# Query chains of a cross-attention, cut in two: three products in one turn of a pair, four in the other

## The chip, the cores and the metric

One core of a Trainium2 chip runs the whole kernel in one launch. The metric is the device time of that launch in microseconds (us). The engines named below work side by side, each in the order of its own instruction queue: PE (matrix products, results in PSUM banks), ACT (ScalarE: copies out of PSUM, exponentials), DVE (VectorE: maxima, reductions, transposes), POOL (GpSimd: elementwise work on SBUF tiles) and SP, which issues the transfers. Differences of under 0.2% are about what a measurement of this kernel cannot tell from no change.

## The reference

The input x is 8 sequences of 224 tokens, 512 wide; the context is 8 sequences of 750 tokens, 384 wide. Three blocks follow each other, each added to x and followed by a layer norm: self-attention with 16 heads, cross-attention with 16 heads of 64, and a gated feed-forward whose weights are rounded to three values. The change lies in the cross-attention:

```python
q = split_heads(x @ Wq)          # 512 -> 1024
k = split_heads(context @ Wk)    # 384 -> 1024
v = split_heads(context @ Wv)
sim = jnp.einsum('bhid,bhjd->bhij', q, k) * SCALE
attn = jax.nn.softmax(sim, axis=-1)
out = jnp.einsum('bhij,bhjd->bhid', attn, v)
return merge_heads(out) @ Wo + bo
```

## The kernel before

The cross-attention runs from about 492 to 1484 us of the span, as 32 turns (`TURNS`, the loop from `for t in range(-1, TURNS)` on; turn -1 only prepares). Eight turns work on a pair of sequences: turn t has pair p = t // 8, a group g of four heads and u = t % 2, the sequence of the pair. An even and an odd turn with the same g share their queries, so they are called a pair of turns here.

In a turn, PE first does the weighted values of the turn before (`weighted`, L1341, tile ov_c), then the scores of this turn (`scores`, L1229, tile sc_c, 24 matrix products, each recorded as two matmuls), then the products for this turn's values (v_x, v_z, v_w, L1090) and the next turn's keys (k_x, k_z, k_w, L1084), interleaved by hand. In this text a turn is counted from its first sc_c matmul to the next turn's first; the weighted values of a turn then lie at its own end. ACT copies scores out of PSUM (L1242), evacuates the products and does the exponentials (L1325), two heads for each of two halves w. DVE takes the maxima of the scores (L1239, L1249 to L1304), subtracts them (L1313), and normalises the turn before (L1249 to L1282 in `inverse_sums`, and L1358). POOL adds up the exponentials (L1328 to L1330) and does the sums within the products (L1122, L1141).

Queries, keys and values are each computed with Strassen-like products of halves: seven products instead of eight, with intermediate sums. `half_steps` writes them as a generator of eight steps, so that the loop can place each step. A product x is copied to m1, then accumulated on and copied to u2, then to u4; z plus m1 is the first block c11; w is copied as c22 (which u4 is added to), goes on to c21 (with u2 added); x ends as c12. The keys' u4 and the queries' u4 are the same buffer, `cku4` (pool `c_sb`, one buffer for each name, `part("k", "u4")`), and the keys' reader of it is the POOL addition at L1141 that makes their c22.

The seven products of the queries (L1097, tiles mq_x, mq_z, mq_w, each product four matmuls in the trace) all stand at the end of each odd turn, for the next two turns. After them comes `ov_c`. Even turns have no query work; their last key step (k_x, then the copy at L1154) stands behind the exponentials in the loop.

Other work is spread over the turns. In turns 0 to 15 ACT sums chunks of the feed-forward weights (L961); from turn 16 on it rounds them (L984), DVE clips them (L990), ACT converts them (L996): one chunk at the opening of each turn and one more at the end of each odd turn, whose conversion follows at the opening of the even turn. From turn 19 and turn 27 on, DVE also normalises finished rows of x (L897, L900). `transpose_x` turns x for the next pair of sequences on PE (L1051) with ACT copies (L1055), in turns 6, 14 and 22; `sum_x` (L1075, four POOL additions) follows it behind `sum_context` (L708). `cross_project` (L262) does the output projection of finished rows in turns 7, 8, 15, 16, 23, 24 and 31.

The PE, ACT, DVE and POOL orders are those in which the code issues (`manual_schedule`); PSUM tiles named "mm" rotate through seven banks. SP's order is chosen by the scheduler.

## Time and profile before

| | us |
|---|---|
| median of 3 runs | 1641.7 (1641.07 to 1641.97) |
| the profiled execution | 1639.92 |
| its span, first to last instruction | 1638.1 |
| turn -1 to the first scores of turn 0 | 492.0 to 507.2 |
| first scores of turn 17, 24, 31 | 1017.0, 1227.7, 1435.3 |
| granted TensorE clock, mean | 0.996 |

The busy shares of the page overlap, since the engines run side by side. [...] In the timeline, a line gives the start, the time, engine, line, operation, output<-inputs, shapes and count; square brackets give the idle time of the engine before it and what ended it.

### The profile page before, as it was taken

How to read it: one execution, taken by the hardware profiler on the slowest of the kernel's cores; microseconds unless marked ns; L12 is line 12 of the kernel's file. 1: busy time of each engine (PE TensorE's matmuls, PEld its weight loads, DVE VectorE, ACT ScalarE, POOL GpSimd, SP SyncE). 2: the span in 40 equal slices, each digit the busy share in tenths (PEclk: the TensorE clock that was granted, in tenths of full speed). 3: DMA queues.
4: the chain of work that ended last, by engine and by line, in shares of the span. 5: the costliest groups of instructions: out<-in, count | busy, mean ns of one | idle time of the engine just before them, and what ended most of it. 6: DMA issues, size and time to landing. Idle time of an engine off the chain costs nothing.

```text
span 1638.1 us, 27155 instructions
## 1 busy us (share of the span) xinstructions
PE 1608.9 (98%) x9682; PEld 1145.7 (70%) x9682; DVE 1341.1 (82%) x2831; ACT 1021.4 (62%) x1874; POOL 934.0 (57%) x861
## 2 busy tenths in 40 slices
PE   8999999999999999999999999999999999999998
PEld 5777676667747877876887876877876877764443
DVE  3999897889956798876889867899987899977877
ACT  5667455556416776755676745776765777746663
POOL 4886575665516564674565664574684474651144
PEclk9999999999999999999999999999999999999999
DMA  8115332424204222330221321231341222413343
GB/s 295 46 52 200 94 121 83 145 77 133 77 1 158 82 62 62 104 107 30 72 88 46 106 80 36 83 101 48 112 131 36 83 89 64 144 45 90 65 91 103
DMA packets 143111, 149.14 MB, mean 91 GB/s; under 512 B 41088, under 2 KB 109184, under 8 KB 142592
## 3 DMA queue, kind: packets, MB, share of 16 engines
q1 hardware_dynamic: 142976, 147.40, 29.4%
q8 instruction: 77, 1.26, 0.3%
q14 instruction: 58, 0.48, 0.1%
HBM read 119.85 MB, written 18.87 MB: 85 GB/s over the span
## 4 chain that ended last, share of the span: by engine, by line
PE 74%; DVE 18%; issue 3%; ACT 3%; POOL 1%; DMA 0%; POOLq 0%; SPq 0%; DVEq 0%; ACTq 0%
PE sc_c L1229 9%; PE ov_c L1341 7%; PE mm_co L262 6%; PE mm_f L1505 6%; PE mm_v L544 5%; DVE cpT L1313 5%; PE q_x L470 5%; PE v_x L1090 5%; PE mm_o L669 4%; PE k_x L1084 4%; PE k_w L1084 3%; PE v_w L1090 3%; PE mq_x L1097 3%; PE q_w L470 2%; PE sc_a L571 2%
## 5 line engine op out<-in xcount | busy, mean ns | idle before, releaser
L1328 POOL TENSOR_TENSOR csh<-cpT 125x672 f32<-125x672 f32 x128 | 210.3, 1643 | 104.6 <-DVE cpT L1313 85.4
L1242 ACT COPY cpT<-sc_c 125x448 f32<-125x448 f32 x384 | 194.9, 535 | 43.0 <-DVE xw L1239 24.0
L200 POOL TENSOR_TENSOR nm_i<-nm_q,mhalf 128x28 f32<-128x28 f32 x32 | 157.9, 4935 | 81.7 <-DVE nm_q L519 81.4
L1313 DVE TENSOR_TENSOR cpT<-cpT,mx_b 125x1344 f32<-125x1344 f32 x128 | 192.6, 1545 | 2.8
L1325 ACT ACTIVATE cpT<-cpT 125x1344 f32<-125x1344 f32 x128 | 170.1, 1329 | 38.7 <-DVE cpT L1313 36.3
L1229 PE MATMUL sc_c<-cq,ckT 64*125 64x224 f32 x1536 | 175.5, 364 | 6.9 <-ACT cpT L1242 6.2
L1122 POOL TENSOR_TENSOR cv<-cv,cvmu 125x384 f32<-125x384 f32 x32 | 31.9, 997 | 263.4 <-ACT cv L1121 252.6
L1229 PEld LDWEIGHTS sc_c<-cq,ckT 64*125 64x125 f32 x1536 | 153.6, 185 | 27.7 <-ACT cpT L1242 14.2
L1341 PE MATMUL ov_c<-cpT,cv 125*64 125x224 f32 x1536 | 158.2, 355 | 2.5 <-ACT cpT L1325 2.5
L1341 PEld LDWEIGHTS ov_c<-cpT,cv 125*64 125x64 f32 x1536 | 109.2, 137 | 52.5 <-issue 8.1
L544 PE MATMUL mm_v<-wv,xnT 128*128 128x512 f32 x224 | 100.4, 592 | 0.0
L1505 PE MATMUL mm_f<-ternary,xqT 128*128 128x512 bf16 x448 | 98.8, 379 | 0.8 <-DVE h L1515 0.8
L262 PE MATMUL mm_co<-xattn_Wo,coT 128*128 128x512 f32 x224 | 97.5, 592 | 0.0
L282 ACT ACTIVATE pr<-sc_a 128x448 f32<-128x448 f32 x120 | 57.9, 535 | 60.4 <-PE sc_a L571 60.1
L1329 POOL TENSOR_TENSOR csm<-csh 125x224 f32<-125x224 f32 x128 | 88.9, 695 | 10.0
L1330 POOL TENSOR_TENSOR csm<-csm,csh 125x224 f32<-125x224 f32 x128 | 84.7, 662 | 10.0
L595 DVE TRANSPOSE_TENSOR_REDUCE sm_q<-pr 128x28 f32<-128x896 f32 x64 | 70.6, 1104 | 19.3 <-ACT pr L282 18.9
L669 PE MATMUL mm_o<-attn_Wo,oT 128*128 128x512 f32 x192 | 84.3, 593 | 0.0
L1239 DVE TENSOR_TENSOR xw<-sc_c,cpT 125x448 f32<-125x448 f32 x64 | 36.9, 617 | 55.0 <-PE sc_c L1229 54.5
L1505 PEld LDWEIGHTS <-xqT 128*128 128x128 bf16 x448 | 43.8, 98 | 54.4 <-issue 2.0
L262 PEld LDWEIGHTS mm_co<-xattn_Wo,coT 128*128 128x128 f32 x224 | 42.4, 190 | 50.8 <-issue 50.1
L554 ACT ACTIVATE v<-mm_v,rms_rs 32x512 f32<-32x512 f32 (+2 forms) x80 | 54.4, 681 | 36.7 <-PE mm_v L544 35.9
(237 smaller groups left out, 3931.3 us busy)
## 6 DMA issues: line engine op xcount, KB each, us to landing
w_slot<-qk_sums SPq DMA_DIRECT2D x22, 512.0 KB, 3.6
xw<-w_sums SPq DMA_DIRECT2D x32, 320.0 KB, 3.0
xwq<-xq_sums SPq DMA_DIRECT2D x16, 512.0 KB, 4.2
w_stage<-w_gateT SPq DMA_DIRECT2D x16, 512.0 KB, 4.7
w_stage<-w_upT SPq DMA_DIRECT2D x16, 512.0 KB, 4.8
w_stage<-w_downT SPq DMA_DIRECT2D x16, 512.0 KB, 4.4
tern<-w_t SPq DMA_DIRECT2D x24, 256.0 KB, 2.5
ternary<-tern SPq DMA_DIRECT2D x3, 2048.0 KB, 7.7
```

The lines of the kernel that those rows point to most:

```text
L200: nc.gpsimd.tensor_tensor(y, v, mhalf.to_broadcast([P, v.shape[-1]]), ALU.pow)
L262: nc.tensor.matmul(mm, lhsT=oT[:, k, c : c + P], rhs=w[:, k, :], start=(k == 0), stop=(k == NPAIR - 1),)
L544: nc.tensor.matmul(mm, lhsT=xnT[:, k, at : at + P], rhs=wv[:, k, c * 512 : (c + 1) * 512], start=(k == 0), stop=(k == KD - 1),)
L669: nc.tensor.matmul(mm, lhsT=joint[g][:, hp, :] if at < 0 else o[:, at : at + P], rhs=wo[:, hp, :], start=(hp == 0), stop=(hp == NPAIR - 1),)
L1090: nc.tensor.matmul(mm[:, t, :], lhsT=c[:, t * CT : (t + 1) * CT], rhs=w, start=start and t == 0, stop=True, skip_group_check=True,)
L1229: nc.tensor.matmul(sc[j][:, i, :], lhsT=kT[h0 : h0 + DH, w, ct * CT : (ct + 1) * CT], rhs=q[h0 : h0 + DH, t % 2, w], start=True, stop=True,)
L1242: nc.scalar.copy(pT[:, j, 2 * c2 : 2 * c2 + 2, :], sc[j])
L1313: nc.vector.tensor_tensor(pT[:, j], pT[:, j], nm[:CT, j] .rearrange("p (o q) -> p o q", o=1) .to_broadcast([CT, NCT, S]), ALU.add,)
L1325: nc.scalar.activation(pT[:, j], pT[:, j], AF.Exp)
L1328: nc.gpsimd.tensor_tensor(half, pT[:, j, 0:3], pT[:, j, 3:6], ALU.add)
L1341: nc.tensor.matmul(ov[h0 : h0 + DH, w, :], lhsT=v[:, ct, hq * DH : (hq + 1) * DH], rhs=pTs[w][:, j, ct, :], start=(ct == 0), stop=(ct == N ...
L1505: nc.tensor.matmul(mm, lhsT=xqTs[i][:, k, :], rhs=w[:, k, cols], start=(k == 0), stop=(k == KD - 1),)
```

## The change

The query chain is divided. `queries_opened` runs in even turns (for the next pair of turns): m1, z and the product that becomes u2, then c11. `queries_closed` runs in odd turns: w (c22), the product u4, c21 and c12. What has to survive from one turn to the next are copies in SBUF: c11 in `cq`, now one tile for the whole stage, and u2, which gets S new columns at the end of the `ctx_even` buffer. Since x is no longer accumulated across the two halves, u2 is added to u4 (one more POOL addition), and to c12 on DVE in place of ACT's copy. The last key step of an even turn moves ahead of the exponentials, as it already was in odd turns. `normalise` becomes a generator of two steps, with the query steps between them. `transpose_x` and `sum_x` move from turns 6, 14, 22 (and `sum_x` from behind the context's sums) to the ends of turns 5, 13, 21. Turn -1 runs both halves, one after the other.

```diff
-                ctx_even = wpool.tile([P, CTX], F32, tag="w", name="ctx_even")
+                ctx_even = wpool.tile([P, CTX + S], F32, tag="w", name="ctx_even")
...
+        cq = sb.tile([P, 2, 2, S], F32, name="cq")
+        u2 = ctx_even[:, CTX:]
...
+        def queries_opened():
+            (a11, a12), _ = xblk
+            m1 = part("k", "m1")[:, :S]
+            x_ = query_bank("mq_x")
+            query_product(x_, a11, b11, True)
+            nc.scalar.copy(m1, x_)
+            yield
+            z_ = query_bank("mq_z")
+            query_product(z_, a12, b21, True)
+            query_product(x_, xsum[:, 1], t2, False)
+            nc.scalar.copy(u2, x_)
+            nc.scalar.copy(cq[:, 0, 0], z_)
+            nc.gpsimd.tensor_tensor(cq[:, 0, 0], cq[:, 0, 0], m1, ALU.add)
+            yield
+        def queries_closed():
+            _, (_, a22) = xblk
+            u4 = part("k", "u4")[:, :S]
+            w_ = query_bank("mq_w")
+            query_product(w_, xsum[:, 2], t3, True)
+            nc.scalar.copy(cq[:, 1, 1], w_)
+            x_ = query_bank("mq_x")
+            query_product(x_, xsum[:, 0], t1, True)
+            nc.scalar.copy(u4, x_)
+            nc.gpsimd.tensor_tensor(u4, u4, u2, ALU.add)
+            nc.gpsimd.tensor_tensor(cq[:, 1, 1], cq[:, 1, 1], u4, ALU.add)
+            yield
+            query_product(w_, a22, t4n, False)
+            nc.vector.tensor_tensor(cq[:, 1, 0], w_, u2, ALU.add)
+            query_product(x_, xsum[:, 3], b22, False)
+            nc.vector.tensor_tensor(cq[:, 0, 1], x_, u2, ALU.add)
+            yield
...
-            query = query_steps(t + 1) if t % 2 and t + 1 < TURNS else iter(())
+            query = iter(())
+            if t % 2 == 0 and t + 2 < TURNS:
+                query = queries_opened()
+            elif t % 2 and t + 1 < TURNS:
+                query = queries_closed()
...
-            if t % 2:
-                next(ks, None)
+            next(ks, None)
+            if t < 0:
+                for _ in queries_opened():
+                    pass
             next(query, None)
             if t >= 0:
                 exponentials(t, 1, pTs[1], (0,))
-            if 1 <= t < TURNS - 1:
-                normalise(t - 1, ov)
+            rest = normalise(t - 1, ov) if 1 <= t < TURNS - 1 else iter(())
+            next(rest, None)
             prior = pTs
-            for _ in range(4):
-                next(query, None)
+            for _ in query:
+                pass
+            for _ in rest:
+                pass
             if t >= 0:
                 exponentials(t, 1, pTs[1], (1,))
-            next(ks, None)
-            for _ in query:
-                pass
             weight_work(t, "late")
             if t % 2 and t + 3 < TURNS:
                 load_queries(place(t + 3)[1])
-            if t >= 0 and t % (2 * QG) == 2 * QG - 2 and t + 2 < TURNS:
+            if t % (2 * QG) == 2 * QG - 3 and t + 3 < TURNS:
                 transpose_x(t // (2 * QG) + 1)
+                sum_x()
...
-                if t % 2 == 0:
-                    sum_x()
```

More of the change, by code (lines that the diff above doesn't have):

```diff
@@ L690, in open_context @@
                 t[:, : KC * SC].rearrange("p (k r s) -> p k r s", k=KC, r=2),
-                t[:, KC * SC :].rearrange("p (i s) -> p i s", i=3),
+                t[:, KC * SC : CTX].rearrange("p (i s) -> p i s", i=3),
             )
@@ L1100, in query_product, with half_steps @@
                 )
-        def half_steps(product, a, b, sums_a, sums_b, dest, part, acc, third=None):
+        def half_steps(product, a, b, sums_a, sums_b, dest, part, acc, third):
             (a11, a12), (_, a22) = a
@@ L1111, in half_steps @@
             c11, c12, c21, c22 = (dest(r, c) for r in range(2) for c in range(2))
-            a13, a23, b31, b32, dif = third or (None,) * 5
+            a13, a23, b31, b32, dif = third
             m1, x_ = part("m1"), acc("x")
@@ L1118, in half_steps @@
             product(z_, a12, b21, True)
-            def corner():
-                nc.scalar.copy(c11, z_)
-                nc.gpsimd.tensor_tensor(c11, c11, m1, ALU.add)
-            if third:
-                product(z_, a13, b31, False)
-                corner()
+            product(z_, a13, b31, False)
+            nc.scalar.copy(c11, z_)
+            nc.gpsimd.tensor_tensor(c11, c11, m1, ALU.add)
             yield
@@ L1133, in half_steps @@
             product(w_, s3, t3, True)
-            if third:
-                product(w_, a23, b32, False)
+            product(w_, a23, b32, False)
             nc.scalar.copy(c22, w_)
@@ L1141, in half_steps @@
             nc.gpsimd.tensor_tensor(c22, c22, u4, ALU.add)
-            if not third:
-                corner()
             yield
             product(w_, a22, t4n, False)
-            if third:
-                product(w_, a23, dif, False)
+            product(w_, a23, dif, False)
             yield
@@ L1151, in half_steps @@
             product(x_, s4, b22, False)
-            if third:
-                product(x_, a13, b32, False)
+            product(x_, a13, b32, False)
             nc.scalar.copy(c12, x_)
@@ L1198, in kv_steps, with query_bank @@
             )
-        def query_steps(t):
-            q = qs_[t // 2] = sb.tile([P, 2, 2, S], F32, name="cq")
-            return half_steps(
-                query_product,
-                xblk,
-                ((wq7[:, 0], None), (wq7[:, 1], wq7[:, 2])),
-                [xsum[:, i] for i in range(4)],
-                [wq7[:, 3 + i] for i in range(4)],
-                lambda u, w: q[:, u, w],
-                lambda n: part("k", n)[:, :S],
-                lambda n: ps_mm.tile([P, S], F32, tag="mm", name=f"mq_{n}"),
-            )
+        cq = sb.tile([P, 2, 2, S], F32, name="cq")
+        u2 = ctx_even[:, CTX:]
+        b11, b21, b22 = (wq7[:, i] for i in range(3))
+        t1, t2, t3, t4n = (wq7[:, 3 + i] for i in range(4))
+        def query_bank(name):
+            return ps_mm.tile([P, S], F32, tag="mm", name=name)
+        def queries_opened():
[29 more added lines that the diff above has]
+            yield
         def scores(t):
-            kT, q = kts.pop(t), qs_[t // 2]
+            kT = kts.pop(t)
             pTs = []
@@ L1231, in scores @@
                                 lhsT=kT[h0 : h0 + DH, w, ct * CT : (ct + 1) * CT],
-                                rhs=q[h0 : h0 + DH, t % 2, w],
+                                rhs=cq[h0 : h0 + DH, t % 2, w],
                                 start=True,
@@ L1261, in spread, with normalise @@
             )
-        def inverse_sums(t):
+        def normalise(t, ov):
+            p, g, u = place(t)
             rc, quarter, res = spread("rc_c")
@@ L1275, in inverse_sums @@
                 nc.vector.reciprocal(res[:Q32, j], tot[:, j::2])
-            for g in range(1, P // Q32):
+            for y in range(1, P // Q32):
                 nc.vector.tensor_copy(
-                    res[g * Q32 : (g + 1) * Q32, g // 2], res[:Q32, g // 2]
+                    res[y * Q32 : (y + 1) * Q32, y // 2], res[:Q32, y // 2]
                 )
+            yield
             for j in range(2):
@@ L1287, in inverse_sums @@
                 )
-            return rc
+            c = (2 * p + u) * S % RING
+            n = min(S, RING - c)
+            for at, q, m in ((c, 0, n), (0, n, S - n)):
+                if m:
+                    nc.vector.tensor_tensor(
+                        oT[:, 2 * g : 2 * g + 2, at : at + m], ov[:, :, q : q + m],
+                        rc[:, :, q : q + m], ALU.mult,
+                    )
+            yield
         def maxima(w):
@@ L1349, in weighted @@
             return out
-        def normalise(t, ov):
-            p, g, u = place(t)
-            rc = inverse_sums(t)
-            c = (2 * p + u) * S % RING
-            n = min(S, RING - c)
-            for at, q, m in ((c, 0, n), (0, n, S - n)):
-                if m:
-                    nc.vector.tensor_tensor(
-                        oT[:, 2 * g : 2 * g + 2, at : at + m], ov[:, :, q : q + m],
-                        rc[:, :, q : q + m], ALU.mult,
-                    )
         def cross_project(i, k0, k1):
@@ L1394, in decoder_block @@
             done.setdefault(t + 1, []).append(i)
-        kts, vs, qs_, outs = {}, {}, {}, {}
+        kts, vs, outs = {}, {}, {}
         pTs = prior = None
@@ L1409, in decoder_block @@
                 if t == TURNS - 1:
-                    normalise(t - 1, ov)
+                    for _ in normalise(t - 1, ov):
+                        pass
                 nm = maxima(1)
@@ L1433, in decoder_block @@
                 exponentials(t, 1, pTs[1], (0,))
-            if 1 <= t < TURNS - 1:
-                normalise(t - 1, ov)
+            rest = normalise(t - 1, ov) if 1 <= t < TURNS - 1 else iter(())
+            next(rest, None)
             prior = pTs
-            for _ in range(4):
-                next(query, None)
+            for _ in query:
+                pass
+            for _ in rest:
+                pass
             if t >= 0:
                 exponentials(t, 1, pTs[1], (1,))
-            next(ks, None)
-            for _ in query:
-                pass
             weight_work(t, "late")
@@ L1479, in decoder_block @@
             cross_project(i, 0, NPAIR - 2)
-        normalise(TURNS - 1, ov)
+        for _ in normalise(TURNS - 1, ov):
+            pass
         for i in last:
```

## The prediction

> **What bounds the kernel now.** I read the page first, for the shares; then a table by turns, for idle PE; then the timeline of the ends of an even turn (10) and an odd one (11), where the edit lies; last the late turns and the granted clock.

> ```profile
> PE 1608.9 (98%) x9682; PEld 1145.7 (70%) x9682; DVE 1341.1 (82%) x2831; ACT 1021.4 (62%) x1874; POOL 934.0 (57%) x861
> ```

> PE is the bound, and the edit removes none of its products: it can only move or end idle time. By turns (10, 11, 20, 21):

> ```profile
> core 0: us, PE busy (x) PEld busy (x) DVE busy (x) ACT busy (x) POOL busy (x), PEclk, DMA share, GB/s
> 800.56:825.59 25.03, 24.77 (x186) 19.55 (x184) 21.17 (x45) 17.84 (x31) 12.48 (x14) 1.00 0.17 53
> 825.59:855.18 29.59, 29.59 (x214) 24.43 (x213) 25.38 (x54) 20.60 (x39) 19.90 (x22) 1.00 0.28 87
> 1102.28:1127.99 25.71, 25.30 (x186) 19.59 (x184) 23.66 (x50) 20.45 (x33) 12.92 (x14) 1.00 0.31 87
> 1127.99:1163.42 35.43, 32.54 (x214) 26.49 (x213) 31.56 (x61) 21.70 (x38) 20.40 (x22) 0.90 0.23 68
> ```

> The even turn is 4.56 us shorter and has an idle PE, the odd one has none. In turns 20 and 21 DVE is nearly full and PE loses far more, with a lower clock. The end of turn 10:

> ```profile
> 818.70 1.43 PE L1084 MATMUL k_x<-ctx_odd,xw 128*128 128x375 f32 x4
> 820.05 2.86 PE L1341 MATMUL ov_c<-cpT,cv 125*64 125x224 f32 x26
> 823.18 2.48 PE L1341 MATMUL ov_c<-cpT,cv 125*64 125x224 f32 x22 [0.26 <-ACT cpT L1325]
> ```

> After 26 matmuls of ov_c PE waits for the last exponential: the starts are 3.13 us apart where 26 times 0.095 is 2.47. That is what three products here would cover. The end of turn 11:

> ```profile
> 845.09 0.92 PE L1097 MATMUL mq_x<-xT,xwq 128*128 128x224 f32 x4
> ...
> 847.05 0.98 POOL L1141 TENSOR_TENSOR ckT<-ckT,cku 128x375 f32<-128x375 f32 x1
> ...
> 849.13 0.35 ACT L1140 COPY cku<-mq_x 128x224 f32<-128x224 f32 x1 [0.47 <-PE mq_x L1097]
> ...
> 850.49 4.76 PE L1341 MATMUL ov_c<-cpT,cv 125*64 125x224 f32 x48
> ```

> Here the POOL line matters: it reads the keys' `cku4` and is done at 848.03, 1.1 us before the queries' u4 copy (L1140) overwrites that buffer. So far nobody waits.

> **Even turns.** From the first score to the end of k_x is 19.40 us (turn 10: 800.56 to 818.70, plus 4 times 0.315). A query product takes 0.756 us (4 starts 0.189 apart), ov_c to the next score 4.69 (850.49 to 855.18), the handover 0.10. So an even turn becomes 19.40 + 3 x 0.756 + 0.10 + 4.69 = 26.46, if nothing waits. Does it? ACT must do, after the first product starts: m1's copy at +1.01 (845.09 to 846.10 in turn 11), the first exponential at +1.26 (1.33 long), u2's and c11's copies (0.25 apart), and the second exponential from about +3.0 to +4.35. PE reaches the matmul that needs it at 2.27 + 0.10 + 2.47 = +4.84. The wait is gone with 0.5 us to spare. Against before: turns 0, 2, 4, 10, 12 (24.98 to 25.03) +7.2 together; turns 6 and 14 (25.93), which lose the transposes, +0.5 each; turns 8 and 16, where the output projection hid the exponentials, the full +2.27 each.

> **Odd turns.** Four products in place of seven: 19.40 + 4 x 0.756 + 0.10 + 4.69 = 27.21. But u4's copy is now second in the chain, not fifth, and the buffer is the same. POOL cannot be earlier: its row of sums starts when the first exponential of the turn ends and runs without a gap to L1141. It ends 2.94 us after the first query product's start in turn 11 (848.03 - 845.09). ACT then copies (0.35, two handovers of 0.05), and PE's fourth product, which accumulates on the bank that is being copied, may start at +3.39 instead of +2.27: a **new wait of 1.1 us** (the same sum gives 1.03 to 1.15 in turns 1 to 19; I take 1.09). Bounds: 0, if POOL is in front; 2.1, if one more POOL addition of 0.98 comes before. I take the row, since the built order keeps the POOL queue as it is up to L1141. Behind the blocked copy stand ACT's two exponentials: they end about 6.05 after the first product; ov_c, itself later, needs them at 3 x 0.756 + 1.09 + 0.76 + 0.10 + 2.47 = 6.7. So one wait, not two. An odd turn becomes 28.30: turns 1 and 9 (29.48) -1.2 each, 3 and 11 (29.59) -1.3, 7 and 15 (36.35, 43.35) -1.2; 5 and 13 gain 16 transposes at 0.109, so +0.5.

> **Small parts.** Turn -1: there u2's copy waited for DVE (PE lost 0.66 at 504.35) and the scores for POOL's c11 (0.33); u2 now has a buffer of its own and c11 is early: -0.95. c12's addition on DVE is 0.38 (row L1149, cq), behind other DVE work that ends 0.5 before the next scores: hidden in early turns, not in late ones. The extra POOL addition (0.66) and c11's lie where POOL is idle 9 us at the start of the next turn; `sum_x` (4 x 1.14) also, in turn 6 (8.9 idle before L1122); without that cover the keys would wait. The reloads of queries: the first two blocks go out after the even turn's products, the sums (4.2 us to landing) after the odd one's and are now wanted some 25 us later instead of 54; SP meets no new wait that others need. Normalising in two steps adds no instruction.

> Sum from turn -1 to the first score of turn 17: -0.95 + 7.2 + 1.0 + 4.5 - 2.4 - 2.6 - 2.4 + 1.0 = **+5.5**.

> **Late turns.** Here DVE and ACT decide when scores leave PSUM:

> ```profile
> 1100.18 1.46 DVE L990 TENSOR_SCALAR w_stage<-w_stage 128x1024 f32<-128x1024 f32 x1
> ...
> 1102.28 4.27 PE L1229 MATMUL sc_c<-cq,ckT 64*125 64x224 f32 x36
> ...
> 1104.86 1.15 DVE L1239 TENSOR_TENSOR xw<-sc_c,cpT 125x448 f32<-125x448 f32 x2
> ```

> The first maximum comes 2.58 us after the first score; undisturbed it is 1.88 (turns 0, 2, 7). The excess is PE's wait. From first maximum to first maximum DVE and ACT need 30.1 in odd turns 17, 19, 27 (their clip waits for nothing that the edit shortens), 25.7 to 28.5 in even ones; odd ones get 0.35 more for c12. PE needs 26.46 and 28.30. So even turns now cover their DVE chain, and odd ones, shorter on PE, run into it: I carry both forward, each first maximum being the later of (first score + 1.88) and (last maximum + DVE's time). Excess: 2.1 (turn 18), 0, 2.2 (20), 2.0 (21, was 3.4), 0.4 (22), 1.0 (23, was 1.5); 2.1 (26), 0, 2.1 (28), 1.0 (29, was 2.4), 1.9 (30), 0.7 (31). Turn 17 to 24: 208.9 against 210.7. Turn 24 to 31: 210.3 against 207.6. Together **+0.9**.

> Clock, in three stretches (the columns of the table by turns; the last but two is the granted clock):

> ```profile
> 1130.16:1133.58 3.41, 1.50 (x14) 1.14 (x12) 3.35 (x6) 0.00 (x0) 1.51 (x2) 1.00 0.00 0
> 1133.58:1136.99 3.41, 2.44 (x13) 2.22 (x14) 2.38 (x5) 3.00 (x6) 0.00 (x0) 0.50 0.00 0
> 1447.60:1451.01 3.41, 1.61 (x15) 1.42 (x15) 3.31 (x3) 2.18 (x3) 0.71 (x1) 1.00 0.00 0
> ```

> After PE gaps of 2.89 us (turn 21) and 1.83 (turn 29) the granted clock was 0.5 for 6.8 and 3.4 us, which cost 2.5 and 1.4 beyond the wait; after 1.80 us (turn 31) it stayed. A gap is the excess less 0.55, so mine are at most 1.65: I count no drop, and these two go (they are in the sums above). If all six excesses of about 2 dropped it, 6 x 1.4 = 8.4 would come on top. [...]

> **Sum.** 1639.9 (profiled execution) + 5.5 + 0.9 = 1646.3; the median shown lies 1.8 above that execution, so 1648.

> **Rivals.**
> (a) *The u4 wait is hidden* (POOL ahead of ACT after all). Then the eight odd turns before 17 save 1.09 each and turn 23 too; the others run into DVE: 1648 - 9.8 = 1638, faster. For: L1141 has never held anyone up. Against: the u4 copy of the built kernel waits for exactly this addition. It decides where POOL's end lies under 1.8 us behind the first query product; it is 2.9. Chance 0.12.
> (b) *The clock drops* in late even turns: up to 1656. For: 1.83 did it. Chance 0.14.
> (c) *Late turns swallow less*: if ACT's lighter odd turns (four copies fewer, 0.25 each) shorten the chain by 0.5 to 1, the six excesses shrink, 3 to 5 less: 1643 to 1645, within 0.2%. Against: at 1100.18 the clip follows DVE's own work. Chance 0.12.
> Forecast as it stands (1645 to 1652): 0.62.

> **The numbers.** Likeliest 1648. The range takes (c), the forecast, and most of (b); (a) and the end of (b) stay out: 1640 to 1656. Within 0.2% is 1638.4 to 1645.0: (c), part of (a), the forecast's edge: 0.19; faster 0.09; slower 0.72.

> **What would show it.** Right: even turns of 26.4 to 26.5 us with no gap in ov_c; odd turns of 28.3 with PE waiting about 1 us before the last mq_x, ended by ACT's u4 copy, and that copy by POOL's ckT; first maxima of turns 18, 20, 26, 28 some 4 us after the first score; no clock below 1 in turns 21 and 29. Wrong: odd turns of 27.2 (a), PEclk under 1 in even late turns (b), late first maxima under 3 us (c).

## The result, and the profile after

The changed kernel takes **1650.6 us** (median of 6 runs, 1650.16 to 1652.34) against 1641.8 (6 runs beside it, 1637.76 to 1642.95): ratio 1.0058, 95% interval 1.0045 to 1.0071. It is slower, by 8.8 us in the medians, and the time lies in the predicted range. Run again later on another chip, beside other runs of the kernel before, it took 1651.5: 1.0070 (1.0055 to 1.0084). The profiled execution took 1650.16, 10.2 more than that of before.

The page's line of the engines, after:

```profile
PE 1603.0 (97%) x9682; PEld 1140.9 (69%) x9682; DVE 1351.7 (82%) x2847; ACT 1014.6 (62%) x1858; POOL 945.3 (57%) x877
```

PE has as many matmuls as before; its share fell, since it idles more (45 us of the span, 29 before). DVE took over 16 copies' worth of work from ACT, and POOL 16 additions more. The table by turns, after (turns 10, 11, 20, 21; columns as before):

```profile
801.73:828.18 26.45, 26.45 (x198) 21.57 (x196) 22.52 (x47) 18.57 (x34) 15.59 (x18) 1.00 0.22 69
828.18:856.58 28.40, 27.47 (x202) 22.30 (x200) 24.40 (x53) 19.46 (x35) 17.52 (x19) 1.00 0.22 71
1107.71:1136.62 28.91, 27.37 (x198) 21.52 (x196) 26.79 (x53) 21.78 (x36) 15.96 (x18) 1.00 0.31 87
1136.62:1169.19 32.57, 29.76 (x219) 24.17 (x217) 30.39 (x60) 21.87 (x38) 19.22 (x21) 1.00 0.22 66
```

The roles have changed places. Turn 10 has no idle PE any more (it had 0.26); turn 11, which had none, has 0.93. Turns 10 and 11 together went from 54.62 to 54.85, turns 20 and 21 from 61.14 to 61.48, although the clock in turn 21 is now full (0.90 before). The end of turn 10, after:

```profile
822.64 0.92 PE L1097 MATMUL mq_x<-xwq 128*128 128x224 f32 x4
823.49 4.76 PE L1370 MATMUL ov_c<-cpT,cv 125*64 125x224 f32 x48
```

All 48 ov_c matmuls now stand in one row: the wait for the exponential is gone. The end of turn 11, after:

```profile
849.53 0.98 POOL L1135 TENSOR_TENSOR ckT<-ckT,cku 128x375 f32<-128x375 f32 x1
850.54 0.34 ACT L1223 COPY cku<-mq_x 128x224 f32<-128x224 f32 x1 [1.66 <-POOL ckT L1135]
...
850.94 1.02 PE L1097 MATMUL mq_x<-xwq 128*128 128x224 f32 x4 [0.93 <-ACT cku L1223]
850.96 0.66 POOL L1224 TENSOR_TENSOR cku<-cku,ctx_even 128x224 f32<-128x224 f32 x1 [0.45 <-ACT cku L1223]
```

This is read backwards: PE's last query product waits for the copy on ACT, which stood idle for 1.66 us until POOL's addition had read the shared `cku4`. POOL in its turn waits 0.45 us for that copy before its next addition. In turns 18, 20, 26, 28 and 30 the first maximum now comes 4.3 us after the first score (2.4 to 2.6 before). The end of turn 17 and the opening of turn 18, whose first score is at 1050.40, after:

```profile
1049.34 1.65 POOL L1357 TENSOR_TENSOR csh<-cpT 125x672 f32<-125x672 f32 x1
1049.63 1.91 DVE L990 TENSOR_SCALAR w_stage<-w_stage 128x1024 f32<-128x1024 f32 x1
...
1051.58 1.15 ACT L996 ACTIVATE w_t<-w_stage,unrounder 128x1024 bf16<-128x1024 f32 x1 [3.31 <-DVE w_stage L990]
...
1052.63 1.23 ACT L984 ACTIVATE w_stage<-w_stage,rounder,wscale 128x1024 f32<-128x1024 f32 x1
...
1053.76 0.51 ACT L1377 COPY ov_s<-ov_c 128x448 f32<-128x448 f32 x1
1053.89 0.69 DVE L990 TENSOR_SCALAR w_stage<-w_stage 128x1024 f32<-128x1024 f32 x1 [2.35 <-ACT w_stage L984]
1054.17 0.96 ACT L1261 COPY cpT<-sc_c 125x448 f32<-125x448 f32 x2
...
1054.32 2.11 PE L1248 MATMUL sc_c<-cq,ckT 64*125 64x224 f32 x12 [1.39 <-ACT ov_s L1377]
...
1054.74 1.16 DVE L1258 TENSOR_TENSOR xw<-sc_c,cpT 125x448 f32<-125x448 f32 x2 [0.15 <-ACT cpT L1261]
```

The clip (L990) takes 1.91 us beside POOL's addition where the next one, alone, takes 0.69. ACT waits for it 3.31 us, then converts, rounds the next chunk, copies ov_c, and only then takes the scores out of PSUM. PE, after 24 score matmuls, waits 1.39 us for that copy of ov_c. So the scores wait for ACT's queue, and that for the clip.

Where the 10.3 us of span went (profiled executions; turn -1 from its first transpose, L1051, the others from first score to first score):

| stretch | predicted | measured |
|---|---|---|
| ahead of turn -1 | 0 | -0.90 |
| turn -1 | -0.95 | -0.97 |
| turns 0 to 16 | +6.3 | +6.93 |
| turns 17 to 30 | +0.9 | +5.42 |
| turn 31 and all after it | 0 | -0.16 |

### The profile page after: what moved, and what is told of

Read it like the earlier page. It is cut to its first block, busy times and chain, and to the rows that moved or that the text cites. A ratio compares the mean times of both kernels' runs of the same rounds, so it can differ in the third digit from the quotient of the medians.

```text
span 1648.4 us, 27094 instructions
## 1 busy us (share of the span) xinstructions
PE 1603.0 (97%) x9682; PEld 1140.9 (69%) x9682; DVE 1351.7 (82%) x2847; ACT 1014.6 (62%) x1858; POOL 945.3 (57%) x877
## 3 DMA queue, kind: packets, MB, share of 16 engines
q8 instruction: 76, 1.25, 0.3%
## 4 chain that ended last, share of the span: by engine, by line
PE 71%; DVE 16%; POOL 6%; ACT 4%; issue 3%; DMA 0%; POOLq 0%; SPq 0%; DVEq 0%; ACTq 0%
PE sc_c L1248 8%; PE ov_c L1370 7%; PE mm_co L262 6%; PE mm_f L1528 6%; PE mm_v L544 5%; PE q_x L470 5%; PE mm_o L669 4%; PE v_x L1090 4%; PE k_x L1084 4%; DVE cpT L1342 3%; PE k_w L1084 3%; PE v_w L1090 3%; PE q_w L470 2%; PE sc_a L571 2%; PE ov_a L640 2%
## 5 line engine op out<-in xcount | busy, mean ns | idle before, releaser
L1357 POOL TENSOR_TENSOR csh<-cpT 125x672 f32<-125x672 f32 x128 | 210.6, 1645 | 108.6 <-DVE cpT L1342 95.7
L1370 PE MATMUL ov_c<-cpT,cv 125*64 125x224 f32 x1536 | 152.9, 355 | 0.3 <-ACT cpT L1354 0.3
```

The source lines that it names most:

```text
L1357: nc.gpsimd.tensor_tensor(half, pT[:, j, 0:3], pT[:, j, 3:6], ALU.add)
L1370: nc.tensor.matmul(ov[h0 : h0 + DH, w, :], lhsT=v[:, ct, hq * DH : (hq + 1) * DH], rhs=pTs[w][:, j, ct, :], start=(ct == 0), stop=(ct == N ...
```

## The experiments

The theory after reading this trace: **A**, two separate losses, the shared `cku4` before turn 17, and in the late turns the clip, which the new additions and delays push into POOL's addition, with ACT's opening queue behind it. Its rivals are named with each run. The expectations are given as they were written ahead of each run. A ratio is always to runs of the kernel before on the same chip.

### 1. u4 in columns of its own

```diff
-                ctx_even = wpool.tile([P, CTX + S], F32, tag="w", name="ctx_even")
+                ctx_even = wpool.tile([P, CTX + 2 * S], F32, tag="w", name="ctx_even")
...
-        u2 = ctx_even[:, CTX:]
+        u2, u4 = ctx_even[:, CTX : CTX + S], ctx_even[:, CTX + S :]
...
-            u4 = part("k", "u4")[:, :S]
```

> The changed kernel, with a buffer of its own for the queries' u4. Theory (the shared buffer makes the odd turns wait for POOL): the last mq_x follows its forerunner by 0.19 us instead of 1.2 to 1.3, odd turns 1, 3, 9, 11 take 27.2 to 27.3 us instead of 28.3 to 28.4. Eight such turns before 17 and turn 23 give 1.1 each, and six late pairs about 0.5 each (POOL's sums come earlier, so the late clip ends earlier), in all about 13: 1638, between 1636 and 1641. The first maxima of turns 18, 20, 26, 28 come 4.8 to 5.0 us after the first score (4.3 now), so the clock may drop there, which would give back 1.4 to 2.5 each. Rival (POOL or ACT is late anyway, and the next wait takes its place): odd turns stay at 28.3, time 1649 to 1651.

Measured 1641.5 us, ratio 1.0014 (1.0005 to 1.0023), just above the range expected. The end of turn 11 with this kernel:

```profile
844.47 0.35 ACT L1222 COPY ctx_even<-mq_x 128x224 f32<-128x224 f32 x1 [0.41 <-PE mq_x L1097]
...
844.75 0.98 POOL L1135 TENSOR_TENSOR ckT<-ckT,cku 128x375 f32<-128x375 f32 x1
```

ACT begins to copy u4 before POOL's addition has even begun; turns 1, 3, 9 and 11 take 27.20 to 27.21 us, as the prediction's sum without the wait had them (27.21). By the end of turn 17 this kernel is 5.6 us ahead of the one before. Then it gives everything back: first maxima at 5.0 to 5.1 in turns 18, 20, 26, 28 and 30, and four clock drops. One of them, in windows (the last column but two is the granted clock):

```profile
1101.68:1105.09 3.41, 1.46 (x10) 1.01 (x10) 3.37 (x6) 3.14 (x6) 0.48 (x1) 1.00 0.66 162
1105.09:1108.50 3.41, 3.25 (x15) 2.51 (x14) 2.38 (x6) 3.15 (x8) 0.00 (x0) 0.50 0.21 71
```

What follows: the buffer is the cause of the wait in odd turns, and it is worth 1.1 to 1.2 us in each. The late turns have a limit of their own: a PE that arrives earlier there only waits longer.

### 2. The whole chain again in odd turns, all else as changed

```diff
+        def queries_whole():
+            yield from queries_opened()
+            yield from queries_closed()
...
-            query = iter(())
-            if t % 2 == 0 and t + 2 < TURNS:
-                query = queries_opened()
-            elif t % 2 and t + 1 < TURNS:
-                query = queries_closed()
+            query = queries_whole() if t % 2 and t + 1 < TURNS else iter(())
```

> The changed kernel with the division alone undone: both halves one after the other in odd turns; snapshots, the shared u4 buffer, the earlier transposes, the earlier key step and the normalising in two steps stay. Theory (the division is what costs): odd turns 29.4 to 29.8 us, even ones 25.0 with the gap of about 0.6 in ov_c back, no wait for u4, first maxima of turns 18, 20, 26, 28 between 2.5 and 3.0 us; time 1639 to 1643. Rival (one of the other parts costs): 1647 or more, with the loss outside the queries.

Measured 1647.5, ratio 1.0049 (1.0032 to 1.0065): not what the theory expected but in the rival's range, so the rest of the change, without the division, costs nearly as much as the whole. It costs elsewhere: turns 0 to 16 take 1.9 us more than before (6.9 with the division), turns 17 to 30 take 7.4 more (5.4). Turn by turn: the early turns are those of before, except that turns 5 and 13 gain 1.7 for the transposes while 6 and 14 give back only 0.9, since the transposes had hidden there the exponential that ov_c waits for (from ov_c to the next scores turn 6 now takes 5.55, before it took 4.69). The turns 18, 20, 26, 28 and 30 have first maxima of 3.2 to 3.3, some 0.7 more than before: with c12 on DVE and one POOL addition more at the end of the odd turn, the clip starts 27.7 us into turn 17 (27.3 before), POOL's long addition 27.4 us into it (26.6 before), and the clip takes 1.90 beside it.

### 3. No late clip

Here the clip of the chunk that is rounded at the end of each odd turn from 17 on is left out (one chunk in three is stored unclipped).

```diff
                     weight_round(*chunks[n + 1], (n + 1) % 2)
-                    weight_clip((n + 1) % 2)
```

> The changed kernel without the clip of the weight chunk that is rounded at the end of each odd turn (a third of the chunks are stored unclipped). Theory (the clip and the conversion behind it hold ACT's score copies at the start of late even turns): first maxima of turns 18 and 26 at 1.9 us instead of 4.3, of 20, 22, 28, 30 between 1.9 and 3.0; turns 18, 26 take 26.5 us; time 9 to 12 less, 1639 to 1642. Rival (the longer even turns themselves, or POOL's later sums, hold the scores): first maxima stay above 4, time within 2 of 1650.

One execution: 1641.0 us, 9.2 under the changed kernel's profiled execution, all of it after turn 17. The opening of turn 18 (first score at 1050.74):

```profile
1048.64 1.15 ACT L996 ACTIVATE w_t<-w_stage,unrounder 128x1024 bf16<-128x1024 f32 x1
...
1052.63 1.16 DVE L1257 TENSOR_TENSOR xw<-sc_c,cpT 125x448 f32<-125x448 f32 x2 [0.75 <-PE sc_c L1247]
```

The conversion now precedes the turn's first score, and the maximum waits for PE (1.89 after the first score) and no longer PE for it. Turns 18 and 26 are undisturbed. Turns 20 and 28 stay at 3.65, above what I expected (1.9 to 3.0): there normalise_x, two rows in 3.8 us, keeps DVE busy.

### 4. One POOL addition more ahead of the keys'

```diff
+                    if n == 4:
+                        nc.gpsimd.tensor_tensor(spare, spare, spare, ALU.add)
```

> The changed kernel with one more POOL addition (128x224, about 0.66 us, on a spare buffer) just ahead of the keys' addition that reads u4. Theory (PE's wait ends with that addition): the step before the last mq_x grows from about 1.25 to 1.9 us in every odd turn, odd turns 1, 3, 9, 11 take 29.0; late pairs lose as much through POOL's later sums; 15 odd turns give about 10: 1659 to 1662. Even turns stay at 26.45. Rival (ACT or PE itself holds the copy): the step stays at 1.25, time within 2 of 1650.

One execution: 1656.5. The end of turn 11, and the end of turn 17:

```profile
853.86 0.56 POOL L1443 TENSOR_TENSOR ctx_even<-ctx_even 128x224 f32<-128x224 f32 x1
...
855.79 1.02 PE L1097 MATMUL mq_x<-xwq 128*128 128x224 f32 x4 [1.44 <-ACT cku L1224]
...
1055.51 0.74 DVE L990 TENSOR_SCALAR w_stage<-w_stage 128x1024 f32<-128x1024 f32 x1
...
1055.77 1.97 POOL L1358 TENSOR_TENSOR csh<-cpT 125x672 f32<-125x672 f32 x1
```

The dose acts: 0.56 us of POOL work lengthens PE's wait by 0.51 (0.93 to 1.44), in every early odd turn. I had expected 1659 to 1662, and missed, because in turns 18, 20, 26, 28 and 30 the first maxima *fell* (turn 18: 4.34 to 2.87). The last two lines show why: POOL's addition now starts 0.26 us after the clip, not 0.29 before it. So the clip takes 0.74 instead of 1.91, and the addition 1.97 instead of 1.65: in each of the two orders it is the one that started second that took longer.

### 5. The clip ahead of the rest of the normalising

If A is right, the clip need not be dropped; it must only come earlier.

```diff
-            for _ in rest:
-                pass
             if t >= 0:
                 exponentials(t, 1, pTs[1], (1,))
             weight_work(t, "late")
+            for _ in rest:
+                pass
```

> The changed kernel, with only the order at the end of each turn altered: the last exponential and the late weight chunk (rounding on ACT, clip on DVE) are issued ahead of the second half of the normalising of the turn before (the transposes and products L1303, L1313); nothing is left out. Theory A (late turns lose because the clip, last on DVE, stands behind POOL's addition, and ACT's conversion of the chunk, its next rounding, the copy of ov_c and the first copy of scores all stand behind the clip): the clip comes some 1.5 to 2 us earlier, ACT's queue at the opening is shorter by as much. First maxima at most 3.0 in turns 18, 26 and 30 (4.34 in the changed kernel) and at most 4.0 in 20 and 28, where normalise_x holds DVE; nothing moves before turn 17. Total 4 to 8 us under the changed kernel: 1643 to 1647. Theory B (DVE's sum of work in odd turns decides, in whatever order): first maxima stay within 0.4 of 4.34 and the total within 2 us of the changed kernel's 1650.6.

Measured 1645.4, ratio 1.0047 (1.0030 to 1.0064). The opening of turn 18:

```profile
1048.59 0.80 DVE L990 TENSOR_SCALAR w_stage<-w_stage 128x1024 f32<-128x1024 f32 x1 [0.72 <-ACT w_stage L984]
...
1049.43 1.15 ACT L996 ACTIVATE w_t<-w_stage,unrounder 128x1024 bf16<-128x1024 f32 x1 [0.87 <-DVE w_stage L990]
```

The clip has moved between two of POOL's long additions (L1357) and takes 0.80 us. First maxima: 2.14 in turn 18, 2.13 in 26, 2.96 in 30; 4.04 in 20 and 4.05 in 28, just above the 4.0 expected, which stay with normalise_x. Both profiled executions are without a clock drop, and their spans differ by 6.7 us (1648.4 and 1641.6). As the ratios' intervals still overlapped, I ran both again side by side:

> The changed kernel unaltered, to have it and the two below on one chip. All theories: 1647 to 1652, ratio to the kernel before 1.0045 to 1.0085, early turns and first maxima as in its first profile. The clock decides within that: an execution whose granted clock is 0.996 should be some 3 us longer than one with 1.0.

> The changed kernel with the late weight chunk ahead of the second half of the normalising, u4 still shared, once more on the chip that runs the changed kernel. Theory A (the clip's place makes the late loss): at equal granted clock 6 to 7 us under the changed kernel, and 3 to 7 in the medians. Theory B (no gain beyond the clock's luck): medians within 1.5 us.

Measured 1651.5, ratio 1.0070 (1.0055 to 1.0084), and 1645.7, ratio 1.0034 (1.0021 to 1.0048): 5.8 us apart in the medians, the intervals now separate. A stands. Of the expected effect of the clock within the changed kernel this group says nothing, since all four of its executions had 0.998; in the first six, the one at 0.996 took 2.0 to 2.2 us more than the two at 1.0, where some 3 were expected.

### 6. The same order in the kernel before

The same five lines moved in the undivided kernel, with its normalising cut in two at the same place.

> The kernel before, undivided, with the same order at the end of a turn: the late weight chunk ahead of the second half of the normalising; nothing left out. It tells whether the order of the clip is worth something by itself or only together with the division. First maxima of turns 18, 20, 26, 30 stand at 2.4 to 2.6, an excess of 0.5 to 0.7 over 1.88; the order can take at most these: 2 to 4 us in all, 1638 to 1640 (ratio 0.9975 to 0.999). The two clock drops in turns 21 and 29 come after even turns, which have no late clip, and should stay. If the total falls by more than 5, the division adds nothing to the order's gain.

Measured 1648.0, ratio 1.0058 (1.0043 to 1.0072): 9.7 us slower, where I had expected 2 to 4 faster. The end of turn 19:

```profile
1098.84 1.26 ACT L984 ACTIVATE w_stage<-w_stage,rounder,wscale 128x1024 f32<-128x1024 f32 x1
...
1100.10 1.64 POOL L1329 TENSOR_TENSOR csh<-cpT 125x672 f32<-125x672 f32 x1
1100.14 2.15 DVE L990 TENSOR_SCALAR w_stage<-w_stage 128x1024 f32<-128x1024 f32 x1 [1.32 <-ACT w_stage L984]
```

With all seven products in the odd turn, ACT ends the rounding only 1.3 us after DVE is free. The clip that DVE waits for still falls behind POOL's addition, by 0.04 us, and now the rest of the normalising stands behind it: the first maxima of turns 20, 22 and 28, which were 2.4 to 2.6, become 4.1 to 4.3, and those of 18 and 26 stay at 2.5. The order gains in the divided chain, whose odd turns leave ACT free sooner: there (experiment 5) the rounding ends 26.3 us into turn 19, here 27.3. I had counted the clip's place on DVE and not the operand that it waits for.

### 7. Both causes removed

> Both causes removed, and nothing left out: u4 has columns of its own and the late clip goes ahead of the second half of the normalising. The early lead of the own buffer at the end of turn 17 (5.6 us under the kernel before) should stand, since nothing moves before turn 17. Theory A: first maxima of turns 18, 26, 30 fall from 5.0 to at most 3.3, no clock drop after turns 18 and 26, so 4 to 9 us less than with the own buffer alone (1641.5): 1632 to 1637, a ratio to the kernel before of 0.994 to 0.998, faster than both kernels. Theory B: late turns give the lead back again, as with the own buffer alone: 1639 to 1642.

Measured **1632.7** us (1631.51 to 1636.61, 7 runs), ratio 0.9967 (0.9954 to 0.9980): faster than both kernels. First maxima: 2.84 in turn 18 (5.03 with u4's own columns alone), 2.82 in 26, but 3.67 in 30, where at most 3.3 was expected. Turns 20 and 28 remain, at 4.8; DVE there, in turn 20, whose first score is at 1094.74:

```profile
1097.40 0.91 DVE L897 TENSOR_SCALAR x<-x,ln_mvs,ln_rss 128x512 f32<-128x512 f32 x1
...
1099.55 1.15 DVE L1257 TENSOR_TENSOR xw<-sc_c,cpT 125x448 f32<-125x448 f32 x2
```

and two clock drops follow them (granted clock 0.50 from 1100.48 and from 1349.65).

### 8. The chain divided in some pairs only

Three variants of the same idea, with u4 in its own columns; the first has the clip last, the other two have it first where the chain is divided.

```diff
+        DIVIDED = (*range(0, 16, 2), 20, 28)
...
-            if t % 2 == 0 and t + 2 < TURNS:
+            if t % 2 == 0 and t in DIVIDED:
...
-                query = queries_closed()
+                query = queries_closed() if t - 1 in DIVIDED else queries_whole()
```

> Own columns for u4, and the chain divided only in the pairs of turns that begin at 0, 2, up to 14, and at 20 and 28; in the other late pairs the whole chain of seven products stays in the odd turn (with c12 still on DVE); the clip stays last. The early turns gain as with the own buffer: 5.6 us under the kernel before at the first score of turn 17. The theory that the division pays where DVE has slack and costs where it has none: turns 18, 26 and 30 then show first maxima of 3.2 as with the whole chain, no clock drop in them; turns 20 and 28 stay near 5.0 with their drop. Total 1636 to 1640, 2 to 5 under the own buffer alone. If the late loss does not come from the division but from c12 on DVE and the moved tail alone, the total equals the own buffer's 1641.5 within 1.5.

> Own columns for u4, the late chunk first, and the chain left whole in the two pairs of turns that begin at 18 and 26, where the odd turn stands ahead of the turns 20 and 28 that normalise_x fills (in these two odd turns the chunk stays last); nothing left out. If the remaining loss of turns 20 and 28 is that the divided odd turn before them is too short for DVE, then 18 is 26.0, 19 30.2 and 20 27.9 long, 84.1 in place of 86.8, and 26 to 28 likewise 84.1 in place of 85.3, with no clock drop after turns 20 and 28: 2 to 5 us under the kernel with all pairs divided (1632.7), so 1628 to 1631, ratio 0.993 to 0.996. If DVE's work in turn 20 itself decides, first maxima stay at 4.8 there and the total at 1632 to 1636.

> The kernel before this one (late chunk first, own columns for u4, chain whole in the pairs of turns that begin at 18 and 26) did the opened half twice in turn -1, because the test for a divided pair failed there: three products too many, 2.73 us with the wait between them (502.25 to 504.97 in its trace), in the path of everything after. Here turn -1 does each half once; nothing else differs. Theory: 2.7 to 3.2 us less than that kernel's 1635.6: 1632.4 to 1632.9, ratio 0.9954 to 0.9960, faster than both kernels, and equal within 1.5 us to the kernel with every pair divided (1632.7, 0.9967): leaving two pairs whole gains in turns 18 to 20 what it loses in 19 and 21. Rival: if turns 20 and 28 were worth the 2 to 5 us expected first, 1629 to 1631.

Measured 1639.7 (ratio 1.0008, 0.9999 to 1.0017), 1635.6 (0.9974, 0.9963 to 0.9985) and 1633.5 (0.9973, 0.9962 to 0.9983). The first two do the opened half twice in turn -1, which was not meant, and the first score of turn 0 came 3 to 4 us later than with all pairs divided. In the first, turns 18 and 26 had first maxima of 3.2 and no drop, as expected, but turns 20 and 28 came out at 3.3 too, where I had expected 5.0: the odd turn ahead of them was whole again. Turn 30, where I had expected 3.2, has 5.08: it follows a divided odd turn. In the second, turns 18 to 20 took 84.0 (84.1 expected; 86.8 with all pairs divided), but 21 and 29 gave 1.1 and 1.3 back. The third has its first score of turn 0 3.1 us earlier, as expected, but 1633.5 is above the 1632.4 to 1632.9 expected, and its ratio did not move (0.9954 to 0.9960 expected): the kernel before ran with fewer clock drops beside it (median 1636.4; see the last section). It stands level with number 7, whose interval holds it. Choosing the pairs shifts the loss and, as far as these runs can tell, does not lower it.

## Why the prediction was right, and where it was not

**Even turns: right.** 26.45 us in turns 0, 2, 4, 6, 10, 12 and 14 (26.46 predicted), with no gap in ov_c; 40.18 in 8, 16 and 24, the full 2.27 more.

**Odd turns: right, with the predicted mechanism.** 28.29 to 28.41 in turns 1, 3, 9 and 11 (28.30 predicted); turns 5 and 13 30.13 and 30.15 (30.04). The chain POOL, ACT, PE was there, with 0.93 us of idle PE in turn 11 and 1.1 to 1.2 us in the length of the turns against experiment 1; experiment 1 removed it with its buffer, experiment 4 lengthened it. So rival (a), that the wait is hidden, is refuted, and its price was wrong as well: it had 1638, faster than before, but with the wait gone the ratio is 1.0014. The late turns took the gain.

**Small parts.** Turn -1 gave -0.97 (14.28 us instead of 15.24; predicted -0.95). That the whole stage began 0.90 earlier, at 491.06 instead of 491.97, is chance: in its second profiled execution the same kernel began it at 492.68. Turns 6 and 14 came as predicted. The terms up to turn 17 add up to +5.35, not to the +5.5 that was written; measured were +5.96 from turn -1 on. `sum_x`, costed at nothing beyond idle POOL, was not free at the end of turn 21. After, at the start of turn 22:

```profile
1169.88 1.13 POOL L1075 TENSOR_TENSOR xwq<-xT 128x448 f32<-128x448 f32 x1
1170.03 1.26 DVE L897 TENSOR_SCALAR x<-x,ln_mvs,ln_rss 128x512 f32<-128x512 f32 x1
```

The normalising step (0.54 alone) takes 1.26 beside it; the first maximum of turn 22 has an excess of 1.69 over 1.88, where 0.4 was predicted.

**Late turns: the mis-sized term, +0.9 predicted, +5.4 measured.** The method, each first maximum from the last one and DVE's time, had the right turns; its excesses were too small in all of them: 2.46 for 2.1 (turn 18), 2.47 for 2.2 (20), 2.40 for 2.0 (21), 1.69 for 0.4 (22), 1.29 for 1.0 (23), 2.46, 2.47, 1.34 and 2.47 for 2.1, 2.1, 1.0 and 1.9 (26, 28, 29, 30). Over turns 18 to 31 the differences add up to 4.3 of the missing 4.5: 1.9 in turns 18, 20, 26, 28 and 30, whose openings stand behind a late clip, and 2.3 in turns 21, 22, 23 and 29, which normalise_x fills. The step that failed is "odd ones get 0.35 more for c12". It added up DVE's own work, and kept the clip's time at 1.46 from the row of before. But the clip's end, which releases ACT's conversion, follows POOL's addition. The end of turn 17, before:

```profile
1043.56 1.65 POOL L1328 TENSOR_TENSOR csh<-cpT 125x672 f32<-125x672 f32 x1
...
1044.30 1.46 DVE L990 TENSOR_SCALAR w_stage<-w_stage 128x1024 f32<-128x1024 f32 x1
```

The clip ends 0.55 us after the addition, here as in the changed kernel (1.46 and 1.91 long). It does so in all 67 cases, in thirteen traces, in which it starts 0.02 to 1.05 us after such an addition, and takes 1.17 to 2.18 us for that. The addition comes 0.73 later in the changed kernel (27.30 us into turn 17 instead of 26.57), and the clip's end 0.72 later, not 0.35; that the clip starts 0.27 later does not count. Of the 0.73, POOL's wait for ACT's copy of u4 (L1224) makes about 0.45: with u4 in columns of its own the addition came at 26.85. The other 0.28 goes with the new order of POOL's additions; no run takes it apart. Experiments 3, 4 and 5 show that the clip behind the addition makes the loss at the openings: it is gone or smaller without the clip, with the addition behind the clip, and with the clip moved ahead. Of the 2.3 us of the other turns only the beginning of turn 22 is shown here; the cause of the rest stays open. I also called it DVE's chain; its end is ACT's opening queue behind the conversion L996.

Clip and addition took 0.74 and 1.97 us in the order of experiment 4, 1.91 and 1.65 in that of the changed kernel. The clip in second place ends 0.55 after the addition, less than its 0.69 alone; no run here shows why, or by what means the two hold each other up.

**Clock: right for the profiled execution, and partly by luck.** No drop in turns 21 and 29. Rival (b) did not come in the median. But PE's wait in turn 21 was 1.85 us, where at most 1.65 was predicted, and in the later run of the same kernel turn 21 had a drop of 6.8 us, which cost 2.7 there, and turn 22 got 1.7 of it back.

**Rival (c), late turns swallow less: refuted.** The lighter ACT did not shorten the chain; it grew.

**The total came near by errors that partly cancel.** The profiled execution grew by 10.2 where 6.4 was predicted (-3.8): the late turns were put 4.5 too low and the early ones 0.5, and the early start of the stage took 0.9 off. The 1.8 us by which I lifted the sum to a median was 0.5 after (+1.3): so 1648 misses 1650.6 by 2.6. That it misses by no more is luck.

## What to carry to other kernels

A step that is moved earlier in its engine's queue moves its *writes* earlier too: look up who still reads the buffer, and what the engine has queued behind the blocked write. A gain for one engine is worth nothing in a stage whose end another chain sets; look for that chain's first link (here a DVE clip behind a POOL addition, with ACT's next turn behind it) before you speed up the rest. Do not carry the duration of a DVE step that overlaps POOL work from one order into another without asking which starts first: here the clip took 0.74 us where it started ahead of POOL's addition, and 1.17 to 2.18 where it started up to 1.05 behind it, with its end 0.55 after the addition's.

## What the hardware showed that I had not expected

```profile
1141.37:1144.79 3.42, 1.59 (x14) 1.18 (x10) 3.39 (x7) 1.46 (x3) 0.00 (x0) 1.00 0.00 0
```

```profile
1138.46:1141.87 3.41, 1.83 (x18) 1.47 (x14) 3.38 (x6) 0.55 (x2) 0.85 (x2) 1.00 0.00 0
```

PE's wait was 1.83 us in the second execution and 1.85 in the first. The second was followed by 6.8 us at 0.5, the first by no drop. So what differed between these two is not how long PE waited (the prediction compared gaps) but how the wait fell on the grid: in the window ahead of the drop PE was busy for 1.59 us of 3.42, in the one without a drop after it for 1.83 of 3.41.

**The spread between executions goes with it.** In the experiments the kernel before ran at 1635.6 to 1637.1 with a mean clock of 0.999, at 1637.6 to 1638.8 with 0.997, at 1639.7 to 1641.0 with 0.996, at 1641.8 to 1643.0 with 0.995. Its median wandered with that (1636.4 to 1641.8 from group to group), so a comparison of a few tenths of a per cent needs many runs of both, or traces of equal clock: the kernel of number 7 at 0.997 stands 5.4 to 6.2 us under the kernel before at 0.997 on the same chip.
